# Three taps of a depthwise convolution on TensorE, for part of the rows of k and v

## The chip, the cores and the metric

The kernel runs on one core of a Trainium2 chip. The metric is the device time of one execution in microseconds (us). The core has five engines that run their own instruction queues in order: TensorE (PE, with its weight loads PEld), VectorE (DVE), ScalarE (ACT), GpSimd (POOL) and SyncE (SP), which issues the DMAs.

## The reference

The input is eight images of 384 channels by 64 by 64, in float32. Two layers each add to the image the output of a block that works on the group-normalised image. The first is a channel attention, whose queries, keys and values pass through a depthwise 3x3 convolution; the second is a selective scan in four directions, followed by a layer norm and a GELU.

```python
q = _dwconv3x3(_conv1x1(x, wq), dwq)
k = _dwconv3x3(_conv1x1(x, wk), dwk)
v = _dwconv3x3(_conv1x1(x, wv), dwv)
q = _l2norm(split(q)); k = _l2norm(split(k)); v = split(v)
attn = softmax(einsum('bhcn,bhdn->bhcd', q, k) * temperature)
out = _conv1x1(einsum('bhcd,bhdn->bhcn', attn, v), wproj)
...
x = x + attention(_gn(x))
x = x + selective_scan(_gn(x))
```

The depthwise convolution multiplies each channel's image by nine weights, one for each shift of a 3x3 window ("taps" 0 to 8; tap 4 is the centre, taps 1 and 7 shift by one row up and down without a shift along the row), and adds the nine products. Outside the image the value is zero.

## The kernel before

Images are worked one after the other: `channel_attention` (L163), then `selective_scan` (L382). Channels lie on the 128 partitions, in three blocks m = 0, 1, 2 of 128; the 64 x 64 pixels of a channel lie along the free dimension, row by row (W = 64 elements a row, L = 4096 in all). The scan takes some 2100 us of each image's 2570 us, the attention some 460.

In the attention, `conv` (L207) makes rows y0 to y1 of one block of q, k or v. For chunks of 8 rows (512 elements[...]) it does the 1x1 convolution as three matmuls (L223) into a tile `pc`, and ScalarE moves it with the bias into the SBUF tile `pre` (L228). Then ScalarE writes the centre tap, `pre` times a weight per channel, to the output (L232), and VectorE adds the eight other taps in place, one instruction each over all rows (L244). The six taps with a shift along the row cover 63 of the 64 columns. Each VectorE instruction depends on the one before, since it adds into the same output.

The order is k (three blocks, the first in two halves), q (three blocks, the last in two halves), then v in three parts of rows (0 to 32, 32 to 48, 48 to 64), each for the three blocks. A finished block of k or q is transposed by TensorE (`to_tokens`, L264; L268) and its squares are summed by ScalarE (`inverse_norm`, L250; L255). For k, VectorE makes a diagonal matrix `diag` of the inverse norms (L284), and TensorE spreads it by one matmul into `pr` (L286). For q, the logits `lg` are masked and go through a softmax (L311 to L322). Between the parts of v stand the projection with the residual (`project_out`, L350) and, from the second image on, the finishing of the image before (`emit`, L329, which calls `finish_part`, L891): loads of the scan's output, ScalarE's normalisation (L900), transposes (L907), the GELU (L908), an addition (L912) and a store.

Buffers set much of the order. In the pool `work`, the tiles `pre` and `acc` (the output of k and q, and the room for finishing parts) have two buffers each, as have `diag` and `lg`. The PSUM tiles `pc` have three buffers, which the projections of q, k, v and of the output share. The program's own order isn't the order of the queues in this part: a planner puts the instructions of the attention on each engine's queue by its own estimate of costs and due times. In the scan, the order is the program's, by `keep_in_program_order`.

## Time and profile before

| what | value |
|---|---|
| median of 3 runs | 20560.08 us (20553.85 to 20561.49) |
| the profiled execution | 20559.6 us, its span 20557.8 us |
| mean granted TensorE clock | 0.968 |
| VectorE's taps in one attention (L244: k, q, v) | 105.6, 106.6 and 113.2 us |
| the attention of image 1 in the trace | 2564 to 3026 us from the span's start |

The span is the time between the first and the last instruction in the trace; the execution's own time has a little around it. A row of the order of time gives start, length, engine, line, operation, output and inputs, shapes and the number of instructions merged into it, and in brackets the idle time of the engine just before, with what ended it. A row that merges several instructions shows the shape of the first of them. One matmul in float32 shows as two records.

### The profile page before, as it was taken

What the parts mean: (1) busy time and instruction counts of PE and PEld (TensorE: products, weight loads), DVE (VectorE), ACT (ScalarE), POOL (GpSimd) and SP (SyncE); (2) the same over time, 40 slices, a digit from 0 to 9 for tenths busy, and PEclk for the clock granted to TensorE, in tenths of its full rate; (3) what the DMA queues carried; (4) which work ended last, traced back from release to release, by engine and by line L of the source; (5) the groups of instructions that cost most, each with busy time, mean ns of one, the idle gap of its engine ahead of it and who ended that gap; (6) DMA issues with size and microseconds to landing.
All of it is one profiled execution on the core that took longest, in us unless ns stands there. A gap on an engine that the chain in (4) does not pass through costs nothing. (4 is left out here: it accounts for less than half of the span.)

```text
span 20557.8 us, 319218 instructions
## 1 busy us (share of the span) xinstructions
PE 19007.6 (92%) x118000; PEld 10494.5 (51%) x118000; DVE 19292.1 (94%) x17310; ACT 17927.7 (87%) x32267; POOL 15434.4 (75%) x6918
## 2 busy tenths in 40 slices
PE   7999979999899998999989999899998999989998
PEld 4555545555455554555545555455554555545554
DVE  8999989999899998999989999899998999989998
ACT  3999949999599995999959998599985999859998
POOL 0999809998199981999819997199971999729997
PEclk8999989999899998999989999899998999989999
DMA  1222322223223232222322223222232222322223
GB/s 40 80 91 93 101 77 82 92 92 100 74 83 92 92 104 69 83 91 92 106 69 83 92 92 104 71 83 92 92 102 72 84 92 92 99 74 84 92 92 117
DMA packets 953162, 1807.94 MB, mean 88 GB/s; under 512 B 125904, under 2 KB 646352, under 8 KB 945456
## 3 DMA queue, kind: packets, MB, share of 16 engines
q1 hardware_dynamic: 950736, 1787.40, 27.1%
q8 instruction: 931, 15.25, 0.3%
q14 instruction: 631, 5.17, 0.1%
q10 hardware_dynamic: 864, 0.12, 0.0%
HBM read 1468.39 MB, written 318.77 MB: 87 GB/s over the span
## 5 line engine op out<-in xcount | busy, mean ns | idle before, releaser
L558 POOL TENSOR_TENSOR db<-w,B 128x1536 f32<-128x1536 f32 x4088 | 14145.7, 3470 | 524.1 <-DVE h L570 193.7
L570 DVE TENSOR_TENSOR_SCAN h<-da,ca,db 128x512 f32<-128x512 f32 x10752 | 13030.9, 1266 | 413.8 <-issue 238.2
L604 ACT ACTIVATE hc<-pt,ct 128x384 f32<-128x384 f32 x15128 | 8430.7, 579 | 237.4 <-PE pt L592 176.4
L549 ACT ACTIVATE da<-dt,neg_a 128x512 f32<-128x512 f32 x12288 | 8509.4, 696 | 100.2 <-DVE h L570 66.9
L592 PE MATMUL pt<-ident,h 128*128 128x128 f32 x49152 | 7978.3, 287 | 524.5 <-ACT hc L604 346.0
L592 PEld LDWEIGHTS pt<-ident,h 128*128 128x128 f32 x49152 | 5143.4, 140 | 5174.3 <-ACT hc L604 2506.3
L621 PE MATMUL py<-hc,pair 128*64 128x384 f32 x24576 | 5328.0, 512 | 9.2 <-DVE ys L692 9.2
L406 POOL MEMSET wdt<- 128x1536 f32 x8 | 11.0, 1378 | 3612.3 <-DMA x1d<-x 3612.3
L570 DVE TENSOR_TENSOR_SCAN h<-da,db 128x512 f32<-128x512 f32 x1536 | 1807.3, 1230 | 129.9 <-ACT da L549 61.2
L628 PE MATMUL py<-hc,pair 128*64 128x128 f32 x24576 | 1897.5, 280 | 0.0
L621 PEld LDWEIGHTS py<-hc,pair 128*64 128x64 f32 x24576 | 1215.4, 135 | 1042.6 <-issue 1042.6
L455 PE MATMUL px<-x,wx 128*44 128x128 f32 x6144 | 1502.6, 338 | 35.3 <-ACT x L421 29.1
L628 PEld LDWEIGHTS py<-hc,pair 128*64 128x64 f32 x24576 | 1403.3, 136 | 252.5 <-issue 248.7
L533 POOL TENSOR_TENSOR w<-x,dt 128x512 f32<-128x512 f32 x744 | 1058.1, 1422 | 0.0
L455 PEld LDWEIGHTS px<-x,wx 128*44 128x44 f32 x6144 | 635.0, 121 | 818.1 <-issue 772.6
L584 POOL COPY ca<-h 128x6 f32<-128x6 f32 x1792 | 348.7, 195 | 699.3 <-DVE h L570 690.5
L606 DVE TENSOR_SCALAR hc<-pt,ct 128x384 f32<-128x384 f32 x1256 | 739.0, 605 | 57.2 <-PE pt L592 15.4
L515 PE MATMUL pd<-xd,wdt 128*128 128x512 f32 x1536 | 747.1, 609 | 44.8 <-ACT hc L604 39.0
L353 PE MATMUL pp<-v,mT 128*128 128x512 f32 x1152 | 557.6, 638 | 124.1 <-DVE v L244 57.3
L525 ACT ACTIVATE dt<-pd,dt_bias 128x512 f32<-128x512 f32 x768 | 474.4, 685 | 19.7 <-PE pd L515 16.0
L515 PEld LDWEIGHTS pd<-xd,wdt 128*128 128x128 f32 x1536 | 275.5, 193 | 327.3 <-issue 187.8
L353 PEld LDWEIGHTS pp<-v,mT 128*128 128x128 f32 x1152 | 230.1, 206 | 405.4 <-issue 316.4
(315 smaller groups left out, 11369.7 us busy)
## 6 DMA issues: line engine op xcount, KB each, us to landing
B<-bcd SPq DMA_DIRECT2D x2048, 512.0 KB
yd<-ys SPq DMA_DIRECT2D x128, 576.0 KB
ys<-yd SPq DMA_DIRECT2D x256, 288.0 KB
yd<-ys SPq DMA_DIRECT2D x256, 288.0 KB
x<-in_x SPq DMA_DIRECT2D x48, 1024.0 KB
x1d<-x SPq DMA_DIRECT2D x192, 256.0 KB
fy<-yd SPq DMA_DIRECT2D x128, 384.0 KB
fin<-yd SPq DMA_DIRECT2D x112, 384.0 KB
```

Of the source, the lines that this page charges most:

```text
L353: nc.tensor.matmul(pc, lhsT=mT[:, j, bass.ts(m, P)], rhs=v[:, j, bass.ts(c, CH)], start=j == 0, stop=j == NJ - 1,)
L455: pin(nc.tensor.matmul(split(pxs[s][:XR, :])[:, part, :], lhsT=wx[:, j, k, :], rhs=view(x1[j], k, c)[:, part, :], start=i == 0, stop=i == ...
L515: pin(nc.tensor.matmul(pds[j], lhsT=wdt[:, k, bass.ts(j, P)], rhs=xds[s], start=True, stop=True))
L533: pin(eng.tensor_mul(split(ws[s][:, j, :]), view(x1[j], k, c), split(dts[s][:, j, :])))
L549: pin(nc.scalar.activation(t, dts[s][:, j, :], AF.Exp, scale=neg_a[:, j, k, n : n + 1]))
L558: pin(eng.tensor_mul(t, ws[g // NP], bts[g][:, v : v + 1, :].broadcast_to([P, NJ, CH])))
L570: pin(nc.vector.tensor_tensor_scan(h, da, db, 0.0 if start else carries[s - 1][:, j, n : n + 1], ALU.mult, ALU.add,))
L592: pin(nc.tensor.transpose(t[:, bass.ts(j, P)], h2s[g][:, j, bass.ts(q, HP), :].rearrange("p l v -> p (l v)"), ident))
L604: pin(eng.activation(out, src, AF.Copy, scale=scale))
L606: pin(eng.tensor_scalar_mul(out, src, scale))
L621: pin(nc.tensor.matmul(py[f * HP : (f + 1) * HP, lb, :C], lhsT=pair, rhs=hc[:, f, :], **flags))
L628: pin(nc.tensor.matmul(py[f * HP : (f + 1) * HP, j, C:], lhsT=pair, rhs=hc[:, f, bass.ts(j, P)], **flags,))
```

## The change

`conv` gets an argument `ys`. Rows y0 to ys are made as before. For rows ys to y1, ScalarE makes three diagonal matrices from the identity, times the weights of taps 4, 1 and 7 (`taps`, one buffer); TensorE multiplies `pre`, shifted by zero, minus one and plus one row, by these matrices and sums the three in PSUM (up to 8 rows at a time, in the tiles `pc`); and ScalarE copies the sum to the output. VectorE's taps 1 and 7 then cover rows y0 to ys alone; its six taps with a shift along the row cover all rows as before, and add into what ScalarE has written. The centre tap's scaling on ScalarE covers rows y0 to ys.

For k, blocks 1 and 2 use ys = 40 of 64 rows. For v, blocks 1 and 2 use ys = 16 in the part of rows 0 to 32. Everything else keeps ys at the end of its rows. The tiles `diag` and `lg` go from two buffers to one.

```diff
-            def conv(which, wt, bias, m, y0, y1, out, edge=None):
+            def conv(which, wt, bias, m, y0, y1, out, edge=None, ys=H):
...
-                o = (y0 - lo) * W
-                nc.scalar.activation(
-                    out, pre[:, o : o + (y1 - y0) * W], AF.Copy, scale=dw[:, m, 4:5]
-                )
+                ys = max(y0, min(ys, y1))
+                if ys > y0:
+                    nc.scalar.activation(
+                        out[:, : (ys - y0) * W], pre[:, (y0 - lo) * W : (ys - lo) * W], AF.Copy,
+                        scale=dw[:, m, 4:5],
+                    )
+                if ys < y1:
+                    taps = work.tile([P, 3, P], F32, tag="taps", bufs=1, name=f"tp{b}{which}{m}_{y0}")
+                    for i, tap in enumerate((4, 1, 7)):
+                        nc.scalar.activation(taps[:, i, :], ident, AF.Copy, scale=dw[:, m, tap : tap + 1])
+                for r in range(ys, y1, CH // W):
+                    e = min(r + CH // W, y1)
+                    pc = ps_c.tile([P, CH], F32, tag="pc", name=f"pd{b}{which}{m}_{y0}_{r}")
+                    for i, dy in enumerate((0, -1, 1)):
+                        r0, r1 = max(r, -dy), min(e, H - dy)
+                        nc.tensor.matmul(
+                            pc[:, (r0 - r) * W : (r1 - r) * W], lhsT=taps[:, i, :],
+                            rhs=pre[:, (r0 + dy - lo) * W : (r1 + dy - lo) * W],
+                            start=i == 0, stop=i == 2,
+                        )
+                    nc.scalar.copy(out[:, (r - y0) * W : (e - y0) * W], pc[:, : (e - r) * W])
...
-                    r0, r1 = max(y0, -dy), min(y1, H - dy)
+                    r0, r1 = max(y0, -dy), min(y1 if dx else ys, H - dy)
+                    if r0 >= r1:
+                        continue
...
-                    conv("k", wk, bk, m, y0, y1, acc[:, y0 * W : y1 * W])
+                    conv("k", wk, bk, m, y0, y1, acc[:, y0 * W : y1 * W], ys=H if m == 0 else 5 * H // 8)
...
-                diag = work.tile([P, P], F32, tag="diag", name=f"diag{b}{m}")
+                diag = work.tile([P, P], F32, tag="diag", bufs=1, name=f"diag{b}{m}")
...
-                lg = work.tile([P, BW], F32, tag="lg", name=f"lg{b}{m}")
+                lg = work.tile([P, BW], F32, tag="lg", bufs=1, name=f"lg{b}{m}")
...
-                    pre = conv("v", wv, bv, m, y0, y1, v[:, m, y0 * W : y1 * W], edges.get(m))
+                    pre = conv(
+                        "v", wv, bv, m, y0, y1, v[:, m, y0 * W : y1 * W], edges.get(m),
+                        ys=H // 4 if y0 == 0 and m > 0 else H,
+                    )
```

## The prediction

> **What bounds the kernel now.** I read the busy table first, then the busy time of each engine in stages of one attention part (image 1, from 2564 to 3026 us), then the order of time of VectorE, ScalarE and TensorE in that part.

> ```profile
> PE 19007.6 (92%) x118000; PEld 10494.5 (51%) x118000; DVE 19292.1 (94%) x17310; ACT 17927.7 (87%) x32267; POOL 15434.4 (75%) x6918
> ```

> Over the whole span three engines look full, but the change touches only the attention part, 462 us of each image's 2570. By stage (columns: window, length, PE, PEld, DVE, ACT, POOL busy with instruction counts, clock, DMA share, GB/s):

> ```profile
> 2649.60:2720.90 71.30, 49.29 (x151) 25.47 (x150) 70.00 (x21) 28.98 (x49) 0.00 (x0) 0.83 0.03 9
> 2720.90:2846.90 126.00, 106.66 (x482) 72.19 (x481) 111.15 (x64) 71.13 (x146) 0.00 (x0) 0.92 0.06 18
> 2846.90:2911.00 64.10, 42.63 (x127) 20.38 (x125) 64.06 (x37) 35.54 (x62) 0.00 (x0) 0.78 0.34 111
> 2911.00:3026.00 115.00, 101.04 (x274) 48.26 (x274) 93.72 (x115) 37.35 (x65) 2.31 (x3) 0.90 0.45 152
> ```

> Blocks 1 and 2 of k (row 1) and the first half of v (row 3) are VectorE's: 70.0 of 71.3 us and all of 64.1 us. Row 4 is mostly TensorE's projection, but what starts it is VectorE's last tap of v, so it moves with VectorE. In the order of time of VectorE the gaps at the seams are short:

> ```profile
> 2649.61 60.98 DVE L244 SCALAR_TENSOR_TENSOR ak<-pre1k,dwk,ak 128x3969 f32<-128x3969 f32 x14 [3.16 <-ACT ak L232]
> 2710.63 4.42 DVE L244 SCALAR_TENSOR_TENSOR ak<-pre1k,dwk,ak 128x4032 f32<-128x4032 f32 x1
> 2720.88 13.20 DVE L244 SCALAR_TENSOR_TENSOR aq<-pre1q,dwq,aq 128x3969 f32<-128x3969 f32 x3 [1.05 <-ACT aq L232]
> 2816.00 2.32 DVE L244 SCALAR_TENSOR_TENSOR aq<-pre1q,dwq,aq 128x2016 f32<-128x2016 f32 x1 [1.74 <-ACT aq L232]
> 2969.59 1.21 DVE L244 SCALAR_TENSOR_TENSOR v<-pre1v,dwv,v 128x960 f32<-128x960 f32 x1
> ```

> The reader is to see that the first tap of k block 1 starts 3.16 us late, released by ScalarE's scaling of the whole block. The other engines at that seam:

> ```profile
> 2645.14 0.69 ACT L228 ACTIVATE pre1k<-pc1k,bias1k 128x512 f32<-128x512 f32 x1
> 2645.86 3.71 ACT L232 ACTIVATE ak<-pre1k,dwk 128x4096 f32<-128x4096 f32 x1
> 2646.66 0.38 PE L286 MATMUL pr<-diag,ones 128*128 128x128 f32 x2
> 2646.88 19.05 PE L223 MATMUL pc1k<-x,wk 128*128 128x512 f32 x44
> 2874.06 10.41 PE L223 MATMUL pc1v<-x,wv 128*128 128x512 f32 x22 [5.76 <-ACT pre1v L228]
> 2879.54 0.93 ACT L228 ACTIVATE pre1v<-pc1v,bias1v 128x512 f32<-128x512 f32 x2 [4.38 <-PE pc1v L223]
> ```

> A 512-column matmul shows as two records, so 44 records in 19.05 us are 22 matmuls of **0.866 us**.

> [...] after 5.76 us idle the next three matmuls, which start at 2874.06, hold ScalarE until 2879.54, some 1.8 us each. [...]

> **The change part by part.** I set the compiled order of the changed kernel's instructions beside the old one. The scan's order, POOL's and the numbers of DMAs are unchanged; on SP only one store of a finished block (fin 5) stands two places later in each image from the second. So all that follows is within attention.

> *Removed on VectorE.* One tap costs per element (4.42 - 1.21) / (4032 - 960) = 1.045 ns. In each of two k blocks tap 1 shrinks from 4032 to 2496 elements and tap 7 from 4032 to 2560: 3008 x 1.045 = 3.14 us, 6.3 for both. In v blocks 1 and 2 of the first half they shrink from 1984 to 960 and from 2048 to 1024: 2.14 us each, 4.3 for both. **Sum 10.6 us per image, 85 us in eight.** This is all on the path.

> *Added on TensorE.* 9 matmuls per k block (9 x 0.866, the last one shorter: 7.7 us) and 6 per v block (5.2), 26 us per image. *On ScalarE.* [...] ten 512-column evictions of about 0.6, while the scaling shrinks from 4096 to 2560 (by about 1.4 us) and from 2048 to 1024 (about 0.85). TensorE and ScalarE have 22 and 42 us free in row 1, so as work this is covered; as latency ahead of VectorE it isn't, because the six taps with a shift cover all rows and the first of them now waits for the last eviction. In detail:

> 1. k block 1. The old chain after the last projection matmul is 0.6 + 3.71, and VectorE starts at 2649.61. Now TensorE's queue holds two tap matmuls, then the norm's matmul pr (waits for diag, so not before 2646.66), then seven more: 2646.88 + 7 x 0.866 = 2652.9, eviction 0.6: start 2653.5. **Loss 3.9 us.** Behind it wait k block 2's projections on TensorE and all taps on VectorE.
> 2. k block 2. TensorE: 2652.9 + 24 x 0.866 (20.8) + 7.7 = 2681.4, eviction until 2682. VectorE is on block 1 until 2653.5 + 31.5 = 2685: covered with 3 us to spare. In the old order the two blocks' taps are interleaved, now they follow each other, so that block 1 is complete 32 us before q's first tap can be wanted instead of 23: the 1.05 us gap goes. **Gain 1.0.** A wait for the norm of block 1 (ScalarE's eight squares end some 11.2 us after it, VectorE asks after 11.4) may cost up to 0.5; I take 0.2.
> 3. q, block 2. ScalarE's order changes: the first square now stands before the last projection's eviction, and a fourth square before the scaling of the second half, two times 0.7 us. VectorE waits for that scaling already (1.74). **Loss 1.4** (0 if that eviction had to wait anyway).
> 4. v block 1. The six matmuls stand among those of the finishing transposes; I get its last eviction at about 2860.1, and VectorE wants the first tap at 2860.0 (five taps and two additions after 2846.9). Loss 0.1, up to 1.
> 5. v block 2. Its projection can start only when block 0's buffer is free (2873.3; now about 1.1 earlier). At half clock 5.3 us, then the six matmuls, then evictions with two finishing activations between: 2884.6 against 2883.9. Loss 0.7; nothing if TensorE is warm, 2 if it stays cold or if the finishing activation waits for its load.
> 6. The diag and lg buffers go from two to one: the next write comes over 20 us after the last read, at no cost; if not, VectorE would wait for pr. SP's store of fin 5 is off the path by the same measure: its buffer is wanted two parts later; bounds 0 to 0.5.

> Per image: 10.6 - 3.9 + 1.0 - 0.2 - 1.4 - 0.1 - 0.7 = 5.3. Bounds: 10.6 with every latency hidden; below 1 with the upper losses together. Image 0 has no finishing work and a gap of 1.67 us at v block 2 already, so I give it 4. Sum 7 x 5.3 + 4 = **41 us**. The profiled execution took 20559.6 us (span 20557.8 and 1.8 around it), 0.5 below the median 20560.08: forecast 20518, 0.20% faster.

> **The rivals.** *All of it arrives.* If TensorE got the seven matmuls done before VectorE was ready, nothing would be lost: 20560 - 85 = 20475. For it: VectorE's 70 of 71. Against: pr in the queue, and that the projection ends only 4.7 us before the old start. Part of it (item 3 nil, item 5 nil) gives 8 x 7.5 = 60: 20500.

> *It is taken back.* The waits at the seams of k, q and v take 4 us per image more: about 20550, no change. For it: item 4 and 5 are ties within a microsecond.

> *Slower: the cold clock.* The place is the tap matmuls ahead of VectorE's first tap at four seams per image. At 1.8 us instead of 0.866 they cost at k 1 seven times 0.93 = 6.5, at k 2 nine times less the 3 spare, 5.4, and at v 12 x 0.93 = 11.2: 23 us per image, against 5.3 gained, so 18 x 8 = 142 us slower: 20702. It decides from an average above about 1.15 us per matmul. Against it: TensorE has been busy up to each of these places but item 5.

> *The change doesn't do what it says* I set aside: the shortened taps (2496, 2560, 960, 1024 elements) and the added matmuls are in the compiled order.

> **How the numbers follow.** 0.2% (41 us) is about what a measurement of this kernel can tell from no change. The worked case (20502 to 20530) gets 0.60, and its centre lies on that bound, so half and a little more of it counts as faster; more of the gain arriving (20470 to 20502) 0.22; taken back (20530 to 20555) 0.12; slower 0.06. Faster 0.36 + 0.22 = 0.58, same 0.24 + 0.12 = 0.36, slower 0.06. The range 20486 to 20550 leaves out the end of the first rival, the end of the second and the third.

> **What would show it.** Right: VectorE's gap ahead of k block 1 grows from 3.2 to about 7 us, released by ScalarE's eviction; k blocks run one after the other in about 63 us; no gap ahead of q's first tap; the gap in q block 2 grows from 1.7 to about 3. Wrong: tap matmuls in records longer than 0.5 us, or a gap over 1 us in the first half of v; or a scan part whose length has changed.

## The result and the profile after

The changed kernel took **20487.7 us** (median of 6 runs, 20479.1 to 20497.6); the kernel before took 20559.2 beside it (6 runs, 20553.9 to 20561.9). That is 71.5 us or 0.35% less; ratio 0.9966, 95% interval 0.9957 to 0.9976. The profiled execution took 20479.1 us, its span 20477.3, and that is 80.5 below the span before. It is the fastest of the six, so what the traces add up to is some 9 us more than the medians show. The forecast was 20518, range 20486 to 20550.

The busy table of the changed kernel (time in us, share of the span, instructions), where VectorE has 81 us less than before and TensorE 140 more:

```profile
PE 19147.7 (94%) x118480; PEld 10548.2 (52%) x118480; DVE 19211.1 (94%) x17310; ACT 17971.1 (88%) x32443; POOL 15434.1 (75%) x6918
```

The busy time of each engine by stage in image 1 of the changed kernel (window, length, PE, PEld, DVE, ACT, POOL, granted TensorE clock, DMA share, GB/s). Row 1 is k blocks 1 and 2 with q's first tap, row 2 the first half of v, row 3 the rest of v and its projection:

```profile
2646.38:2710.40 64.02, 62.13 (x183) 29.93 (x181) 63.70 (x20) 31.32 (x57) 0.00 (x0) 1.00 0.03 9
...
2838.44:2900.00 61.56, 48.36 (x154) 23.26 (x153) 61.45 (x39) 38.07 (x72) 0.00 (x0) 0.91 0.37 115
2900.00:3006.00 106.00, 95.47 (x260) 43.88 (x258) 90.50 (x104) 34.29 (x60) 2.31 (x3) 0.96 0.48 163
```

In k TensorE is now as full as VectorE, 62.1 and 63.7 of 64.0 us. VectorE's order of time at the seams of k:

```profile
2646.38 43.70 DVE L264 SCALAR_TENSOR_TENSOR ak<-pre1k,dwk,ak 128x3969 f32<-128x3969 f32 x11 [7.16 <-ACT ak L252]
2690.00 0.15 DVE L278 TENSOR_REDUCE rnk<-rpk 128x1 f32<-128x8 f32 x1
...
2706.29 4.34 DVE L264 SCALAR_TENSOR_TENSOR aq<-pre1q,dwq,aq 128x3969 f32<-128x3969 f32 x1
2710.55 4.34 DVE L264 SCALAR_TENSOR_TENSOR ak<-pre1k,dwk,ak 128x3969 f32<-128x3969 f32 x1
2714.82 8.80 DVE L264 SCALAR_TENSOR_TENSOR aq<-pre1q,dwq,aq 128x4032 f32<-128x4032 f32 x2
```

The gap ahead of k block 1 is 7.16 instead of 3.16 us, released by the eviction of a tap sum (L252). The gap ahead of q is gone. A single record of a tap matmul lasts 0.59 us, as it overlaps the next; from start to start it is 0.43, so the records are to be counted by the row. TensorE and ScalarE at that seam:

```profile
2637.72 1.88 PE L247 MATMUL pd1k<-pre1k,tp1k 128*128 128x512 f32 x4
2639.44 0.38 PE L306 MATMUL pr<-diag,ones 128*128 128x128 f32 x2
2639.66 6.07 PE L247 MATMUL pd1k<-pre1k,tp1k 128*128 128x512 f32 x14
2645.56 20.76 PE L224 MATMUL pc1k<-x,wk 128*128 128x512 f32 x48
```

```profile
2645.76 0.58 ACT L252 COPY ak<-pd1k 128x512 f32<-128x512 f32 x1 [1.88 <-PE pd1k L247]
2646.25 0.99 ACT L241 ACTIVATE tp1k<-ident,dwk 128x128 f32<-128x128 f32 x3
```

**Where the 80.5 us lie.** I took the times of the same instructions in both traces and added the differences of the stretches over the eight images:

| stretch | change, us in eight images |
|---|---|
| start to the first tap | +1.4 |
| k's first part, to the first tap of block 1 | +32.4 |
| from there to q's second tap | -59.2 |
| q, to v's first tap | +17.2 |
| v, to its last tap | -34.2 |
| *attention, to v's last tap* | *-43.7* |
| from v's last tap to the scan's first product w (final projection, group norm) | -23.9 |
| the scan, to the next image | -14.3 |

So the attention gives about the worked sum (41), and **38 us come from stretches in which the change alters no instruction**. In the first of these, the matmuls of the changed kernel are faster. TensorE's order of time of image 1 from v's last tap on, before:

```profile
3003.12 13.47 PE L353 MATMUL pp<-v,mT 128*128 128x512 f32 x24 [7.17 <-DVE v L244]
3020.18 3.15 PE L136 MATMUL pv<-var,avg 128*128 128x1 f32 x14 [0.84 <-DVE var L131]
3026.93 5.35 PE L455 MATMUL px<-x,wx 128*44 128x128 f32 x24 [3.61 <-ACT x L421]
```

and after:

```profile
2990.89 12.45 PE L373 MATMUL pp<-v,mT 128*128 128x512 f32 x24 [7.17 <-DVE v L264]
3006.92 1.83 PE L136 MATMUL pv<-var,avg 128*128 128x1 f32 x14 [0.84 <-DVE var L131]
3012.35 4.20 PE L478 MATMUL px<-x,wx 128*44 128x128 f32 x24 [3.60 <-ACT x L444]
```

The idle time ahead of them is the same (7.17, 0.84, 3.60); the three groups together are 3.5 us shorter. The stages cut at the changes of the granted clock (the third column from the right) say why. Before:

```profile
2998.80:3009.04 10.24, 5.92 (x7) 2.52 (x8) 7.26 (x9) 0.00 (x0) 0.00 (x0) 0.50 0.29 105
3009.04:3019.28 10.24, 9.11 (x32) 4.84 (x30) 6.21 (x11) 0.00 (x0) 2.31 (x3) 1.00 0.36 127
3019.28:3032.93 13.65, 8.55 (x39) 7.62 (x38) 8.58 (x25) 6.39 (x9) 0.00 (x0) 0.50 0.04 11
```

and after:

```profile
2987.91:2994.74 6.83, 3.85 (x5) 1.81 (x6) 4.20 (x6) 0.00 (x0) 0.00 (x0) 0.50 0.31 98
2994.74:3008.39 13.65, 11.68 (x47) 6.72 (x47) 8.51 (x17) 0.00 (x0) 2.31 (x3) 1.00 0.39 135
3008.39:3015.22 6.83, 3.23 (x17) 2.88 (x17) 4.80 (x14) 5.22 (x8) 0.00 (x0) 0.50 0.00 0
```

### The profile page after: what moved, and what is told of

It is laid out like the page before. It is cut to its first block, busy times and chain, and to the rows that moved or that the text cites. A ratio compares the mean times of both kernels' runs of the same rounds, so it can differ in the third digit from the quotient of the medians.

```text
span 20477.3 us, 320345 instructions
## 1 busy us (share of the span) xinstructions
PE 19147.7 (94%) x118480; PEld 10548.2 (52%) x118480; DVE 19211.1 (94%) x17310; ACT 17971.1 (88%) x32443; POOL 15434.1 (75%) x6918
## 5 line engine op out<-in xcount | busy, mean ns | idle before, releaser
L538 PE MATMUL pd<-xd,wdt 128*128 128x512 f32 x1536 | 749.6, 611 | 44.6 <-ACT hc L627 38.8
```

The lines of the kernel that those rows point to most:

```text
L538: pin(nc.tensor.matmul(pds[j], lhsT=wdt[:, k, bass.ts(j, P)], rhs=xds[s], start=True, stop=True))
```

## The experiments

From here on, w is the scan's first product, and the grid is the row of places, 3.413 us apart, on which all changes of the clock in a trace lie. Three theories. **A**: the worked sum, and beyond it a TensorE that the added matmuls keep warmer. **B**: time follows the VectorE work taken away; the clock is no part of it. **C**: the extra 38 us depend only on where the 3.413 us grid falls relative to v's last tap. From the delayed kernels on, A stands for the plain sum of the stages, without the clock.

All medians, each beside the kernel before (20559.2 for the changed kernel, 20561.9 for the next four, 20564.8 for the four after them, 20557.7 for the last four), with the changes in the trace (eight images, against before). A trace is of one execution, which lies up to 10 us off its median. The start of the first image, up to 4.3 us, is in neither of the two last columns:

| kernel | median, us | against before | ratio, 95% interval | attention | after v's last tap |
|---|---|---|---|---|---|
| changed kernel | 20487.7 | -71.5 | 0.9957 to 0.9976 | -43.7 | -38.2 |
| k alone | 20518.3 | -43.5 | 0.9971 to 0.9988 | -17.3 | -26.6 |
| v alone | 20533.1 | -28.8 | 0.9979 to 0.9992 | -28.6 | -2.3 |
| matmuls alone | 20611.4 | +49.5 | 1.0014 to 1.0034 | +63.6 | -7.8 |
| k block 2 only, 40 rows | 20481.6 | -80.3 | 0.9949 to 0.9974 | -62.8 | -7.8 |
| before, 1 delay | 20568.1 | +3.3 | 0.9993 to 1.0010 | +14.6 | -11.4 |
| before, 2 delays | 20591.0 | +26.2 | 1.0006 to 1.0020 | +31.7 | +4.7 |
| changed, 1 delay | 20531.8 | -33.0 | 0.9977 to 0.9990 | -27.9 | -5.5 |
| k block 2, v 24 rows | 20462.3 | -102.6 | 0.9938 to 0.9962 | -83.0 | -14.8 |
| before, warmed | 20529.8 | -27.9 | 0.9980 to 0.9993 | +3.8 | -32.7 |
| changed, warmed | 20479.9 | -77.7 | 0.9949 to 0.9974 | -37.4 | -37.6 |
| k block 2, v 24 rows, warmed | 20443.2 | -114.5 | 0.9932 to 0.9959 | -75.4 | -38.8 |
| the same, v 32 rows | 20458.4 | -99.3 | 0.9940 to 0.9965 | -67.6 | -36.8 |

**The two halves of the change.** The changed kernel with one of the two places put back:

```diff
-                        ys=H // 4 if y0 == 0 and m > 0 else H,
+                        ys=H,
```

> The changed kernel with v as before: only blocks 1 and 2 of k have rows on TensorE. Theory A (the worked sum holds up to v's last tap, and what the total shows beyond it is TensorE's clock after attention): from the landmarks of the changed kernel, k's first tap of block 1 comes 4.0 us later per image, q's first tap 3.4 us earlier than that would give twice over (-7.4), q loses 2.1; k and q together win about 10 us in eight images, and 0 to 15 more if TensorE is warmer in the later part: 20535 to 20550. Theory B (the whole gain is VectorE time taken away, spread by instructions removed): k removes 6.3 of 10.6 us per image, so 0.59 of 72 us: about 20517. Theory C (the extra is where the half-clock windows happen to fall): anything within 30 us of 20549, with the extra not tied to the k part.

```diff
-                    conv("k", wk, bk, m, y0, y1, acc[:, y0 * W : y1 * W], ys=H if m == 0 else 5 * H // 8)
+                    conv("k", wk, bk, m, y0, y1, acc[:, y0 * W : y1 * W], ys=H)
```

> The changed kernel with k as before: only the first half of v's blocks 1 and 2 has rows on TensorE. Theory A: v's last tap comes 34 us earlier over eight images, and all of it reaches the end: 20525, less up to 38 if the warmer transition to the scan comes with v's matmuls. Theory B: v removes 4.3 of 10.6 us per image, 0.41 of 72 us: 20530. Theory C: within 30 us of 20525, in either direction. The two parts alone add up to the whole (72) in B; in A they add up to about 44 plus the clock's share.

By their totals these two speak for B: 43.5 and 28.8, as B said (45 and 32), and they add up to 72.3. The stretches say otherwise. In the attention k wins only 17.3 us and v 28.6, the reverse of B's shares and in the order of A's (about 10 and 34); k's total is made up by 26.6 us after v's last tap. The sum fits by chance. Neither total tells the theories apart.

**The matmuls without the saving.** Tap matrices, matmuls and evictions stay at their places, but go to a spare tile; VectorE and the scaling do all the work as before:

```diff
+                    spare = work.tile([P, JUNK], F32, tag="junk", bufs=1, name=f"sp{b}{which}{m}_{y0}_{r}")
+                    nc.scalar.copy(spare, pc)
-                    nc.scalar.copy(out[:, (r - y0) * W : (e - y0) * W], pc[:, : (e - r) * W])
```

> The kernel before with every tap matmul, tap matrix and eviction of the changed kernel at the same places, their result unused; VectorE makes all nine taps as before. Theory A with warmth (the added 26 us of matmuls per image keep TensorE's clock up after attention): attention itself is longer where the tap matmuls delay VectorE or share the queue (k's seam +4 per image less what no longer waits for the eviction, so 0 to 30 us), and the parts from v's last tap on are shorter by about 38 us as in the changed kernel: 20520 to 20555. Theory B (VectorE time alone): nothing is gained, 20560 to 20600. Theory C (phase of the clock's windows): the parts after v change by up to 30 us with either sign.

After v's last tap it wins 7.8 us, not 38, though the added matmuls are the same: 26 us more matmuls per image don't by themselves warm what comes later in the image. A's reason for the extra falls. Its attention is 63.6 us longer, more than expected, and that is mostly the kernel's own order: VectorE's gap ahead of q in image 1,

```profile
2738.45 8.81 DVE L261 SCALAR_TENSOR_TENSOR aq<-pre1q,dwq,aq 128x3969 f32<-128x3969 f32 x2 [8.28 <-ACT aq L232]
```

comes from TensorE, which could not begin q until ScalarE had evicted the unused sums of block 2:

```profile
2709.51 20.31 PE L223 MATMUL pc1q<-x,wq 128*128 128x512 f32 x40 [2.92 <-ACT sp1k L251]
```

So this run says nothing of what the tap matmuls cost in k.

**The seam at k block 1 undone.** Block 1 is VectorE's again, block 2 gets 40 rows on TensorE:

```diff
-                    conv("k", wk, bk, m, y0, y1, acc[:, y0 * W : y1 * W], ys=H if m == 0 else 5 * H // 8)
+                    conv("k", wk, bk, m, y0, y1, acc[:, y0 * W : y1 * W], ys=3 * H // 8 if m == 2 else H)
```

> The changed kernel with block 1 of k all on VectorE again and 40 rows of block 2 on TensorE (24 in the changed kernel, in both blocks). The tap matmuls of block 2 lie under block 1's taps, so no first tap should wait for them. Theory A: the 7.2 us gap ahead of k block 1 is back at 3.2 (32 us in eight images), k block 2 gives 40 x 64 x 2 x 1.045 ns = 5.35 us per image (43 in eight) in the place of 6.3 (50): some 25 us better than the changed kernel, 20463, with the clock's share as there. Theory B (time follows the work taken from VectorE): 1 us less per image, 8 us worse, 20496. Theory C: 20463 with 30 to either side.

In the attention it is 19 us better than the changed kernel, somewhat less than the 25 expected. VectorE and TensorE in image 1:

```profile
2647.31 54.44 DVE L264 SCALAR_TENSOR_TENSOR ak<-pre1k,dwk,ak 128x3969 f32<-128x3969 f32 x13 [3.17 <-ACT ak L234]
```

```profile
2644.58 19.05 PE L224 MATMUL pc1k<-x,wk 128*128 128x512 f32 x44
2663.47 12.93 PE L247 MATMUL pd1k<-pre1k,tp1k 128*128 128x512 f32 x30
```

The gap is back at 3.17, and 15 tap matmuls lie wholly under block 1's taps. Yet the total is only 6 to 9 us better by the medians (20481.6, where A had 20463), and 11 us worse between the two profiled executions, because after v's last tap it wins 7.8 us instead of 38.2. Work saved and time saved have come apart. C says where the difference went: from v's last tap to w its images 1 to 7 take 34.4 us on average, those of the changed kernel 32.3.

**A delay as a probe.** From v's last tap to w every kernel so far issues the same instructions. I took for each image the place of v's last tap in the grid (time since the last grid edge) and the time from there to w. With the delayed kernels below, 70 images of ten kernels (images 1 to 7, none warmed) fall in these groups:

| place in the grid, us | images | v's last tap to w, us |
|---|---|---|
| 0.97 to 1.80 | 18 | 32.1 to 32.6 |
| 1.90 to 2.68 | 20 | 33.3 |
| 2.69 to 2.73 | 3 | 34.6 |
| 2.84 to 3.41 and 0 to 0.83 | 29 | 35.4 to 35.9 |

In the profiled executions all seven images of before are in the last group, all seven of the changed kernel in the first. They stay there since the last taps of images 1 to 7 follow each other in a nearly whole number of grid steps: 2556.6 us before (749.0 steps), 2546.3 after (746.0). Where the executions without a trace lay isn't recorded. To cause it rather than see it, I added one VectorE instruction per image where VectorE has no idle time:

```diff
+                if which == "v" and m == y0 == 0:
+                    for i in range(1):
+                        late = work.tile([P, 1], F32, tag="late", bufs=1, name=f"late{b}_{i}")
+                        nc.vector.reduce_max(late, out[:, :1600], axis=AX.X)
```

> The kernel before with one more VectorE instruction per image, a maximum over 1600 elements of v's block 0 after its first-half taps, result unused, about 1.7 us, in a stretch where VectorE has no idle time. Theory A (time is the sum of the stages, the clock no part of it): 8 x 1.7 = 13.6 us slower, 20575. Theory C (the clock of TensorE changes only at the edges of a grid of 3.413 us that runs through the whole program, and the 35.6, 33.3 or 32.2 us from v's last tap to the scan's first product depend on where in the grid v's last tap falls): before has all of images 1 to 7 in the 35.6 case; 1.7 us per image moves them through the grid, some into the shorter cases. From the pooled seven images of six kernels: 0 to 4 us slower, 20562 to 20566.

> The kernel before with two of these instructions per image, about 3.4 us, one whole step of the grid. Theory A: 27 us slower, 20589. Theory C: the images are back in the case they were in (35.6 us), so nearly the whole delay shows, 17 to 27 us: 20579 to 20589; the first instruction costs little and the second most of it.

> The changed kernel with the same added VectorE instruction, about 1.7 us per image. Theory A: 13.6 us slower than the changed kernel, 20501. Theory C: the changed kernel has all of images 1 to 7 in the 32.2 us case, which the delay takes them out of: 20 to 30 us slower, 20508 to 20518, twice what the instruction itself takes.

The groups of the kernel before with one delay show its cost:

```profile
L251 DVE TENSOR_REDUCE late<-v 128x1 f32<-128x1600 f32 x8 | 14.5, 1811 | 0.0
```

The same 14.5 us of work cost 3.3 us in the kernel before, some 23 more when added a second time (20559.7 to 20575.0 against 20584.1 to 20600.0), and 38 to 44 in the changed kernel (20522.3 to 20538.6; the first number takes each median against its own before). The interval of the first, 0.9993 to 1.0010, would allow 14.5 too; there the trace decides. The two delays together (26.2) fit A's 27 as well as C. The attention is 14.6 us longer, and 11.4 are given back after v's last tap, where images 1 to 6 have moved to 32.2 (one) and 33.3 us (five). With two delays six of seven images are back at 35.6; in the changed kernel five of seven have gone from 32.2 to 35.4 or more. The last cost more than the 20 to 30 that C expected, and far more than A's 13.6: of its 32.7 us after v's last tap, 12.2 lie in the scan.

**Taking the idle time away.** TensorE idles for 7.17 us ahead of the last projections, which wait for v's last tap. Eight matmuls of no use fill this time:

```diff
+            warm = ps_a.tile([P, CH], F32, tag="pa", name=f"warm{b}")
+            for i in range(8):
+                nc.tensor.matmul(warm, lhsT=ident, rhs=pre[:, :CH], start=True, stop=True)
             for t in todo:
                 project_out(*t)
```

> The kernel before with eight more matmuls of 512 columns per image (6.9 us at 0.866), result unused, placed where TensorE has its 7.2 us of idle time ahead of v's last tap, just before the last row of projections. Theory A (the clock is no part of it): they lie in idle time, no change, 20565. Theory C: without the idle time the windows after it are not at half clock; the last 12 projection matmuls take 10.4 instead of 13.5 us and at best the two short groups after them lose 2.4 more, so v's last tap to the scan's first product takes 32.2 or less instead of 35.6: 3.4 to 5.5 us in each of seven images, 24 to 38 us faster, 20527 to 20541, with no VectorE instruction taken away.

> The changed kernel with the same eight matmuls. Theory A: no change. Theory C: it has the 32.2 us case already in all images, so there is little left, 0 to 2 us per image from the projection matmuls (12.45 instead of 10.4): 0 to 14 us faster than the changed kernel. If both warmed kernels are in the same case, the difference between them is the change's own share without the clock's: about 42 us (theory C) in the place of 71.5.

The kernel before, with nothing taken from VectorE, is 27.9 us faster, as C expected (24 to 38); the changed kernel gains 6 to 8 (0 to 14). TensorE in image 1 of the first:

```profile
2989.15 7.03 PE L380 MATMUL warm<-pre1v,ident 128*128 128x512 f32 x16
2996.02 5.31 PE L353 MATMUL pp<-v,mT 128*128 128x512 f32 x12
3001.63 10.54 PE L353 MATMUL pp<-v,mT 128*128 128x512 f32 x24 [0.30 <-DVE v L244]
```

The same 24 records take 10.54 us, 13.47 before and 12.45 in the changed kernel. From 2989.00 to 3012.00, a stretch in which TensorE is busy for 22.70 of 23.00 us, the granted clock is 1.00; before it was 0.70 in the 7.17 us of idle time and 0.78 in the 13.47 us of matmuls. The time from v's last tap to the group norm's mean is 14.67 us in all images 1 to 7 of both warmed kernels; without the matmuls it was 16.1 to 17.7, by the place in the grid. The stretches behind the mean still depend on the place: up to w it is 30.3 to 31.9 us. With both warmed, the change is worth 49.9 us by the medians (42 were expected) and 46.4 by the traces: 41.2 in the attention, 0.2 at the start, 4.9 after v's last tap. So of the 71.5, the 41 us of the attention are the change's own; the rest comes from the stretches behind v's last tap, and most of it goes with the grid.

**A better version.** I joined the two better places and gave v's blocks 1 and 2 more rows:

```diff
-                        ys=H // 4 if y0 == 0 and m > 0 else H,
+                        ys=H // 8 if y0 == 0 and m > 0 else H,
```

> The kernel with 40 rows of k block 2 on TensorE and k block 1 all on VectorE (its time was 20481.6), and in the first half of v 24 instead of 16 of the 32 rows of blocks 1 and 2 on TensorE. Theory A: two taps of two blocks lose 512 elements each, 2.1 us per image, 17 in eight; three more matmuls and an eviction per block are 3.2 us of latency at seams that had a tie, so between 17 faster and 30 slower, about 20482. Theory C: as A for attention, and from v's last tap on up to 25 us either way by where the grid falls.

> The kernel with 40 rows of k block 2 and 24 rows of v's blocks 1 and 2 in the first half on TensorE (20462 on its own) and the same eight matmuls. Theory A: no change. Theory C: its images 1 to 7 lie in all three cases, 33.2 us on average, so 1.0 to 3 us per image: 7 to 21 us faster, 20441 to 20455.

> The same with all 32 rows of v's blocks 1 and 2 in the first half on TensorE. Taps 1 and 7 are gone from VectorE there, 2 x 2 x 512 elements less, 2.1 us per image, 17 in eight, if TensorE keeps up (three more matmuls and an eviction per block, 3.2 us of latency ahead of a block's first tap); 24 instead of 16 rows brought about 20. If the seams are now late, 3 us per block are lost and it is 20 to 30 us slower than with 24 rows.

24 instead of 16 rows of v brought 19 to 22 us, a little more than the most expected (17), and the warming 12 to 19 more (7 to 21 expected). With both it takes **20443.2 us** (20442.2 to 20452.4), 0.55% less than before and the best of all. With 32 rows v block 2 is too late: VectorE waits ahead of block 2 in image 1,

```profile
2871.69 2.25 DVE L264 SCALAR_TENSOR_TENSOR v<-pre1v,dwv,v 128x1953 f32<-128x1953 f32 x1 [5.03 <-ACT v L252]
```

and 15 us are lost (20455.7 to 20466.1), less than the 20 to 30 expected of late seams.

## Why the prediction was right, and where it wasn't

- **The sum, 41 us: right for what it covered**, 43.7 in the attention of the trace and 41.2 between the warmed kernels. Two misses within it nearly cancel: q lost 0.75 us per image more than worked out, v 0.8 less. That the total (71.5) still fell in the range, less than 2 us from its end, is luck: the lower end stood for another reason, "more of the gain arriving".
- **Removed VectorE work**, 10.6 us per image: arrived whole where nothing waited. From the first tap of k block 1 to q's second tap the sum had 6.3 + 1.0 - 0.2 = 7.1; measured 7.4. The wait for the norm (0.2) didn't come: the reduction in `rnk` at 2690.00 has no gap.
- **Item 1, k block 1 late, 3.9**: measured 4.05 per image. The queue is as worked out: two tap matmuls, `pr`, seven more, an eviction. A tap matrix took 0.33 us (three in 0.99).
- **Item 3, q block 2, 1.4**: measured 2.15 per image up to v's first tap. The scaling's gap grew by 0.6, as far as 2.32; the other part I had not seen. The logits wait for `pa` 1.4 us longer:

```profile
2804.20 0.36 DVE L332 TENSOR_TENSOR lg<-pa,rks 128x192 f32<-128x192 f32 x1 [3.54 <-PE pa L325]
...
2807.91 2.32 DVE L264 SCALAR_TENSOR_TENSOR aq<-pre1q,dwq,aq 128x2016 f32<-128x2016 f32 x1 [2.32 <-ACT aq L234]
```

  With block 1 back on VectorE these gaps are 2.13 and 1.88, near the 2.13 and 1.74 of before, and q loses 0.2 per image, so most of the loss belongs to block 1's rows on TensorE. With k alone it is 1.4 per image; the kernel before with a delay in v, whose q is the same, also varies by up to 0.6, so the other 0.7 isn't explained. I have not split which of the moved instructions does it.
- **Items 4 and 5, v, 0.8**: nothing. v won 4.27 of 4.3 us per image. In image 1, the half clock that item 5 counted on came, but for one grid step only. TensorE's projection of block 2 (six records of 512 columns, then six of 64), the tap matmuls, and the clock:

```profile
2864.53 5.15 PE L224 MATMUL pc1v<-x,wv 128*128 128x512 f32 x12 [4.08 <-ACT pre1v L229]
2869.51 5.37 PE L247 MATMUL pd1v<-pre1v,tp1v 128*128 128x512 f32 x12
```

```profile
2865.03:2868.45 3.42, 3.42 (x5) 1.35 (x4) 3.42 (x3) 1.64 (x3) 0.00 (x0) 0.50 0.20 66
```

  The three matmuls of 512 columns took 4.4 us instead of the 5.3 of before, where the granted clock was 0.52 from 2874.06 to 2879.54. The last eviction ends at 2875.51 and VectorE comes to block 2 at 2875.77, so a loss of 0.7 became a spare time of 0.3.
- **Item 6, the single buffers of `diag` and `lg`**: nothing, as worked out. The kernel with v alone has them too, and its k and q take as long as before (2.0 us more in all eight images together).
- **The step that failed** is "So all that follows is within attention". The instructions after it are the same, their times are not. I had read the half clock as a cost at single places, the price of an idle time (5.76 us in the trace of before, ahead of v's block 2); it is also a state that whole images share, and a shift of some microseconds per image moves all of them to another place in the grid. Behind v's last tap the forecast had no change; the trace has 38.2 us. "A scan part whose length has changed" was named as a sign against the prediction, and it appeared (14.3 us).
- **The rivals.** "All of it arrives" (20475) is near the total, but its mechanism is refuted by the 7.16 us gap. "Taken back" didn't happen. The cold clock as a loss didn't either: the clock of row 1 is 1.00, and the 14 records of tap matmuls ahead of k block 1 took 6.07 us, 0.43 each. The sign "records longer than 0.5 us" was badly chosen, since a single record lasts 0.59 at full clock too.

**Still open:** the scan's 14.3 us, which no experiment separated. The traces show where most of it lies. In each of images 1 to 7 of before, the clock is at half for one more grid step some 26 us after w; no image of the changed kernel has this step. Image 1 before, and the same part of the scan after:

```profile
3063.65:3067.06 3.41, 3.41 (x13) 1.19 (x10) 2.60 (x3) 1.44 (x3) 2.93 (x2) 0.50 0.01 2
```

```profile
3042.53:3056.00 13.47, 11.99 (x77) 6.19 (x75) 12.78 (x12) 10.62 (x18) 11.22 (x7) 1.00 0.12 40
```

Between the scan's steps on either side of this place (the 13th and the 31st scan instruction of VectorE) the changed kernel wins 10.4 of the 14.3 us. Over 84 images of all kernels, the time from w to the next image's first tap is 2119.2 us on average in the 38 images with this step and 2117.6 in the 46 without it. The two groups overlap, so it isn't the only cause.

## What to carry to other kernels

When a change saves more than the work it removes, compare the traces stretch by stretch, ahead of any story: here nearly half of the gain in the trace lay where nothing had been changed. A kernel that repeats the same work many times can sit in one position of TensorE's clock grid in all repetitions (before, images 1 to 7 were 749.0 grid steps apart), so that its time goes in steps: the same 14.5 us cost 3 in one kernel and about 40 in another, and differences of 0.2% between two versions aren't the worth of the edit until the grid is ruled out. If TensorE idles just ahead of matmuls that others wait for, try filling the idle time with spare matmuls: here, with 7.17 us of idle time, that took much of the position out of the measurement (from v's last tap to w 30.3 to 31.9 us, instead of 32.1 to 35.9), and was faster, by 27.9 us in the kernel before and by 6 to 8 in the changed one.

## What the hardware showed that I had not expected

- The three main positions of the grid give 32.2, 33.3 and 35.6 us for the same instructions, a spread of 3.4 us, just one grid step. In seven images that is 7 x 3.4 = 24 us, 0.12% of the time, but a third of this change.
- Eight unneeded matmuls per image, 56 us of TensorE time in all, made the kernel before 27.9 us faster.
